# A cross-attention kernel: the order of small steps in its first and last batch

## The chip, the cores and the metric

The kernel runs on one core of a Trainium2 chip. A core has TensorE (PE in the profile; its weight loads are PEld), VectorE (DVE), ScalarE (ACT), GpSimd (POOL) and SyncE (SP); SP only issues DMAs, and ACT and POOL issue some too. All are in-order queues that wait for one another by semaphores. The metric is the device time of one execution in microseconds (us); the median of the runs counts.

## The reference

There are 8 batches; in each, x1 and x2 have 512 channels and 1024 positions, all in float32.

```python
q = jnp.einsum('bcn,dc->bnd', x1, Wq) + bq
k = jnp.einsum('bcn,dc->bdn', x2, Wk) + bk[:, None]
v = jnp.einsum('bcn,dc->bdn', x2, Wv) + bv[:, None]
attn = jax.nn.softmax(jnp.einsum('bnd,bdm->bnm', q, k), axis=2)
attn_out = jnp.einsum('bcm,bnm->bcn', v, attn)
return attn_out + x1
```

Here d is 64. The shapes of Wq and Wk are 64 x 512, that of Wv is 512 x 512.

## The kernel before, in words

**The algebra.** The kernel does not form v. It computes y = x2 times the transposed exponentials of the scores, divides each column by its sum of exponentials, and multiplies by Wv; bv and x1 are added at the end. Both large products are done by seven half-size products instead of eight (the scheme of Strassen and Winograd). The left factor x2 is cut into blocks A11, A12, A21, A22, which are loaded transposed (`load_a`), and four sums S1 to S4 are formed from them (`sum_a`, `left_sums`, `L110`); S3 overwrites A21 and reads A11. The right factor, the exponentials, is cut into blocks "11", "12", "21", "22" with the sums T1 to T4 (`sum_e`, `L262`); T3 overwrites block "12". The products are numbered 1 to 7 (`MULT`). In most batches some of the products 2, 3, 4 and 7 are themselves done by seven smaller products (`inner_left`, `inner_right`, `inner_product`); their sums are at `L355` and `L367`. For product 4 the right inner sums (tile `eI4eT`) are formed from T4. The results of the first stage are y blocks 11, 12, 21, 22 (`evict_y`, `multiply_3` for block 12); the second stage multiplies them with Wv (`second(i)`), and `evict_o` adds bias and x1 and stores.

**The softmax.** Scores lie with keys on the 128 partitions and queries along the row. Half h of the queries has four pairs of score tiles (`scores(s, h, i)`, a pair covering both halves of the keys). Score tiles go from PSUM to SBUF by ScalarE (`L198`, `L200`); the maximum over keys is folded on VectorE (`fold`, `L211`; the two halves at `L215`) and then taken over the partitions by GpSimd (`highest`, `L221`). The subtraction of the maximum is VectorE's (`L243` in the first half of the first batch, `L249` elsewhere), the exponential is ScalarE's (`L244`, `L253`). The sums over keys are folded in the same way (`sums`, or by accumulating DMAs in later batches, `L555`), and reduced over partitions by GpSimd in `total` (`L226`); the reduced row is then brought by a small DMA to a tile `few`, `shares` takes its reciprocal (`L234`), writes it to DRAM (`L236`) and reads it back to all partitions (`L238`) as `rden`.

**The order.** The order of instructions on each engine is written out by hand: `head(s)` prepares the first batch, `head_second` its second half of queries, and `period(s, n, nn, nnn)` does one batch `s` while it prepares the batches `n`, `nn`, `nnn` behind it. In the first batch `s.b == 0`; in the last one `n` is None. Buffers are few: `x` is a single buffer that x1 and x2 of the coming batches take in turn, so a load waits until the queries or keys made from the one before are done. PSUM has two tiles "sc" for scores and inner products and the banks a0, a1, c0, c1 for the large products. Each queue is in order: for example SP issues x2 of batch 1 (`load_x`, `L126`) and then A11 of batch 1 (`load_a`, `L133`).

**T4.** In batches 0 and 1, T4 is formed on VectorE. In the others ScalarE copies block "21" (`L278`) and two DMAs from GpSimd's queue add T2 to the copy (`L280`).

**The last batch.** Near its end stand product 7, product 3 with the eviction of block 12 (`evict_3`: `L452`, then `L483`, which frees the banks a0, a1), and product 4, whose right inner sums (`inner_right(s, 4, ...)`, `L367`) are formed on VectorE after `evict_3`. In `multiply_onto` the first step of product 4 takes T4 itself, the second (number 7) takes the third of these sums.

Of the kernel before, what the change touches and what calls it, by code (L numbers as in the profile page):

```python
# [11 lines left out]
ALU = mybir.AluOpType  # L12
# [3 lines left out]
def kernel(  # L16
# [53 lines left out]
    MH = N // P // 2  # L70
# [64 lines left out]
    def sum_a(s, *ks):  # L135
        for k in ks:
            if k != "S3":
                s.a[k] = sb.tile([P, MH, C // 2], F32, tag=f"a{k}", name=f"a{k}_{s.b}")
        left_sums(s.a, *ks)
# [35 lines left out]
    def scores(s, h, i, bank=None):  # L175


        if i == 0:
            s.e[h] = sb.tile([P, 2, MH, H], F32, tag=f"e{h}", name=f"e_{s.b}_{h}")
        e = s.e[h]  # L180
        if bank:
            whole = None
            ps = [
                ps_a.tile([P, H], F32, tag=f"{bank}{g}", name=f"ps_s{bank}{g}_{s.b}_{h}_{i}")
                for g in range(2)
            ]
        else:
            whole = ps_s.tile([P, 2, H], F32, tag="sc", name=f"ps_s_{s.b}_{h}_{i}")
            ps = [whole[:, g, :] for g in range(2)]
        for g, r in ((0, lo), (1, hi)):  # L190
            nc.tensor.matmul(  # L191
                ps[g], s.k[r, ts(i, P)], s.q[r, ts(h, H)], start=True, stop=True
            )

        def copy():
            if bank:
                for g in range(2):
                    nc.scalar.copy(e[:, g, i, :], ps[g])  # L198
            else:
                nc.scalar.copy(e[:, :, i, :], whole)  # L200

        copy.ps = ps
        return copy

    def fold(s, h, i, kind, op):

        e = s.e[h]
        if i == 1:
            s.mx[h] = sb.tile([P, 2, H], F32, tag="fold", name=f"{kind}_{s.b}_{h}", bufs=2)
        f = s.mx[h]  # L210
        nc.vector.tensor_tensor(f, e[:, :, 0, :] if i == 1 else f, e[:, :, i, :], op)  # L211
# [59 lines left out]
    def sum_t4(s):  # L271

        s.t["T4"] = t4 = sb.tile([P, MH, H], F32, tag="eT4", name=f"eT4_{s.b}")
        if s.b < 2:
            sum_e(s, "T4")
            return
        for i in (0, 2):
            nc.scalar.copy(t4[:, i : i + 2, :], s.t["21"][:, i : i + 2, :])  # L278
        for i in (0, 2):
            nc.gpsimd.dma_start(t4[:, i : i + 2, :], s.t["T2"][:, i : i + 2, :], accum_op=ALU.add)  # L280
# [328 lines left out]
    def head(s):  # L609

        s.q = sb.tile([P, N], F32, tag="q", name=f"q_{s.b}", bufs=2)
        s.k = sb.tile([P, H], F32, tag="k", name=f"k_{s.b}", bufs=2)
        x1_sb = sb.tile([P, CT, N], F32, tag="x", name="x1_head")
        x2_sb = sb.tile([P, 2, MH, H], F32, tag="e1", name="x2_head")
        s.x = x2_sb.rearrange("p a (b t) n -> p (a b) (t n)", t=2)  # L620

        def load_x1(c, h):
            nc.sync.dma_start(
                x1_sb[:, c : c + 2, ts(h, H)],
                x1[s.b, c * P : (c + 2) * P, ts(h, H)].rearrange("(t p) n -> p t n", p=P),
            )

        nc.gpsimd.dma_start(bqk_sb, bqk)
        nc.gpsimd.dma_start(bv_sb, bv)
        nc.scalar.dma_start(wqk_sb, wqk)  # L630
        warm = const.tile([P, P], F32, name="warm")
        nc.vector.memset(warm, 0.0)
        ps = ps_a.tile([P, H], F32, tag="a0", name="ps_warm")
        for _ in range(WARM):
            nc.tensor.matmul(ps[:, 0:P], warm, warm, start=True, stop=True)
        load_x1(0, 0)
        load_x1(2, 0)
        for n in HALVES:
            for c in range(CT):
                to, of = (  # L640
                    x.rearrange("p (h n) -> p h n", h=2)[:, :, n]
                    for x in (s.x[:, c, :], x2[s.b, ts(c, P), :])
                )
                nc.sync.dma_start(to, of)
        nc.scalar.activation(warm[:, 0:1], warm[:, 0:1], AF.Exp)
        load_x1(0, 1)
        load_x1(2, 1)
        load_a(s, "21", "22", "11", "12")
        load_values()
        tiles = range(CT)  # L650
        head_queries(s, x1_sb, 0, "c1")(*tiles)
        head_keys(s, left, "c0")(*tiles)
        more_keys = head_keys(s, right, "a0")
        more_keys(0)
        s.mx[0] = f = sb.tile([P, 2, H], F32, tag="fold", name=f"max_{s.b}_0", bufs=2)
        copies = [scores(s, 0, i) for i in range(2)]
        for g in range(2):
            nc.scalar.copy(s.e[0][:, g, 0, :], copies[0].ps[g])
            nc.vector.tensor_tensor(f[:, g, :], s.e[0][:, g, 0, :], copies[1].ps[g], ALU.max)
        fold_halves(s, 0, ALU.max)  # L660
        more_keys(*tiles[1:])
        copies[1]()
        more_queries = head_queries(s, x1_sb, 1)
        more_queries(0)
        for i, bank in ((2, "a"), (3, "c")):
            copy = scores(s, 0, i, bank)
            for g in range(2):
                nc.vector.tensor_tensor(f[:, 0, :], f[:, 0, :], copy.ps[g], ALU.max)
            copy()
        highest(s, 0, halves=False)  # L670
        sum_a(s, "S1", "S2")
        more_queries(*tiles[1:])
        load_x(states[1], x1)
        copies = [scores(s, 1, 0), scores(s, 1, 1), scores(s, 1, 2, "c")]
        for g in range(2):
            for i in range(MH):
                first_exponentials(s, g, i)
        for copy in copies:
            copy()
        fold(s, 0, 1, "sum", ALU.add)  # L680
        fold(s, 0, 2, "sum", ALU.add)
        fold(s, 1, 1, "max", ALU.max)
        fold(s, 0, 3, "sum", ALU.add)

    def head_second(s, n):


        scores(s, 1, 3)()
        for i in range(2, MH):
            fold(s, 1, i, "max", ALU.max)  # L690
        queries(n)
        load_x(n, x2)
        highest(s, 1)
        sum_a(s, "S3", "S4")
        for i in range(MH):
            exponentials(s, 1, i)

# [10 lines left out]
    def period(s, n, nn, nnn):  # L708
# [15 lines left out]
        if s.b == 0:  # L724
            head_second(s, n)
        sum_e(s, "T1", "T2")
        if s.b < 2:
            total(s, 0)
        else:
            shares(s, 0)  # L730
        if n:
            load_a(n, "11")
        if s.b == 0:
            first(2)
            evict_y(s, "11", (1,))
            keys(n)
            load_x(nn, x1)
            sum_t4(s)
            sums(s, 1)
            shares(s, 0)  # L740
        else:
            evict = multiply_2(s)
            sums(s, 1)
            evict()
            if s.b == 1:
                shares(s, 0)
            sum_t4(s)
            sum_a(s, "S4")
# [37 lines left out]
        if seven:  # L786
            hooks = [{}, {}]
            if n:
                for i in range(MH):
                    lower(n, 0, i)  # L790
                hooks = [
                    {
                        1: lambda: copy_first(n, 0),
                        6: lambda: add_exponential(1),
                        5: lambda: add_exponential(2),
                    },
                    {6: lambda: add_exponential(3)},
                ]
            first(5, (lambda: exponential(n, 0, 0)) if n else None)
            inner_right(s, 3, s.t["22"], "eT1")  # L800
            inner_left(s, 4, s.a["22"], "a12")
            add_7 = multiply_7(s, hooks[0])
            add_7()
            evict_3 = multiply_3(s, hooks[1])
            evict_y(s, "22", (1,))
            evict_3()
            inner_right(s, 4, s.t["T4"], "eT2")
        else:
            first(5)
            if s.b == 0:  # L810
                inner_right(s, 3, s.t["22"], "eT1")
                for i in range(MH):
                    lower(n, 0, i)
            else:
                for i in range(MH):
                    exponentials(n, 0, i)
                start_sum(n, 0)
                inner_right(s, 3, s.t["22"], "eT1")
            first(7)
            if s.b > 1:  # L820
                inner_right(s, 4, s.t["T4"], "eT2")
            evict_3 = multiply_3(s, {})
            if s.b:
                evict_y(s, "22", (1,))
                evict_3()
            else:
                evict_3()
                evict_y(s, "22", (1,))
# [105 lines left out]
```

## Time and profile before

| what | us |
|---|---|
| median of 3 runs | 693.46 (693.18 to 695.86) |
| the profiled execution | 693.62 |
| its span, first to last instruction | 691.8 |
| busy: TensorE / VectorE / ScalarE / GpSimd | 682.8 / 628.9 / 276.1 / 193.5 |
| TensorE's wait for product 4's sums, last batch | 2.3 |
| reductions over partitions: maximum (`L221`, 16 of them) | 1.74 to 2.69, median 2.15 |
| reductions over partitions: sum (`L226`, 16 of them) | 3.18 to 7.54, median 3.98 |

Times in the profile are microseconds from the start of the span. A row of a timeline gives start, duration, engine, line, operation, the tile that is written and those that are read, and, in brackets, how long the engine was idle before it and who ended that. "Landing" is the time from the issue of a DMA until its data are there. The granted clock of TensorE was 1.00 throughout.

### The profile page before, as it was taken

Reading aid. Unit: us, or ns where it says so; the run is one execution under the profiler, and the core shown is the slowest. Engines: PE = TensorE matmul, PEld = TensorE weight load, DVE = VectorE, ACT = ScalarE, POOL = GpSimd, SP = SyncE. Lnnn points to the kernel's source line nnn. Section 1 sums busy time; section 2 is a strip of 40 time slices with the busy share of each in tenths; the row PEclk is TensorE's granted clock in tenths of the full one; section 3 lists DMA queues with packets and bytes.
Section 4 is the critical chain, followed back from the end, with each engine's and each line's share of the span. In section 5 each row is a group of like instructions: output and inputs, shape, how many; then the busy total and the mean of one; then the engine's idle time right before and its main releaser. Section 6 shows DMA issues by size and latency. Waiting matters only on the chain.

```text
span 691.8 us, 6647 instructions
## 1 busy us (share of the span) xinstructions
PE 682.8 (99%) x2248; PEld 364.2 (53%) x2248; DVE 628.9 (91%) x809; ACT 276.1 (40%) x439; POOL 193.5 (28%) x147
## 2 busy tenths in 40 slices
PE   9999999999999999999999999999999999999997
PEld 5333554535545565455644566454754545545753
DVE  1999999988999889998999989999799988999785
ACT  2733353146233552345432454424544245243220
POOL 0123113522423223242142321623223232323000
PEclk9999999999999999999999999999999999999999
DMA  9676256954569754786628867198642864268303
GB/s 304 258 214 238 65 182 130 255 161 79 183 114 235 199 106 153 150 231 181 135 111 180 230 181 187 42 198 215 167 92 38 207 166 76 62 148 223 87 0 122
DMA packets 44723, 109.05 MB, mean 158 GB/s; under 512 B 4880, under 2 KB 7184, under 8 KB 44688
## 3 DMA queue, kind: packets, MB, share of 16 engines
q1 hardware_dynamic: 25856, 70.13, 30.1%
q0 software_dynamic: 17424, 36.25, 29.7%
q10 hardware_dynamic: 1408, 2.23, 1.0%
q8 instruction: 18, 0.29, 0.2%
q14 instruction: 17, 0.14, 0.1%
HBM read 72.62 MB, written 16.81 MB: 129 GB/s over the span
## 4 chain that ended last, share of the span: by engine, by line
PE 93%; DMA 3%; DVE 1%; SPq 1%; ACT 1%; issue 0%; DVEq 0%
PE ps_ya L321 24%; PE ps_i L374 17%; PE ps_oa L321 16%; PE ps_oc L321 12%; PE ps_s L191 6%; PE ps_yc L374 5%; PE ps_q L149 4%; PE ps_k L149 3%; PE ps_yc L321 3%; PE ps_ya L374 3%; DMA a<-in_x2T_dram 1%; DMA x_in_x_dram<-in_x_dram 1%; DMA x_head<-in_x_dram 1%; PE ps_sc L191 1%; PE ps_sa L191 1%; DVE aS L110 0%
## 5 line engine op out<-in xcount | busy, mean ns | idle before, releaser
L321 PE MATMUL ps_ya<-eT,aS 128*128 128x512 f32 x256 | 113.1, 595 | 0.0
L332 ACT COPY uy<-ps_ya 128x512 f32<-128x512 f32 x48 | 28.1, 588 | 139.6 <-PE ps_ya L321 126.7
L249 DVE TENSOR_TENSOR e<-e,top 128x1024 f32<-128x1024 f32 x60 | 70.5, 1228 | 11.0 <-POOL top L221 11.0
L321 PEld LDWEIGHTS ps_ya<-eT,aS 128*128 128x128 f32 x256 | 48.0, 190 | 60.9 <-issue 58.5
L253 ACT ACTIVATE e<-e 128x1024 f32<-128x1024 f32 x60 | 62.9, 1059 | 38.6 <-DVE e L249 37.1
L221 POOL PARTITION_ALL_REDUCE top<-max x16 | 32.8, 2052 | 150.8 <-DVE max L215 78.9
L226 POOL PARTITION_ALL_REDUCE den<-sum x16 | 63.4, 3961 | 40.8 <-DVE sum L215 35.8
L321 PE MATMUL ps_oa<-yT,w_S 128*128 128x512 f32 x128 | 57.6, 593 | 0.0
L321 PE MATMUL ps_oc<-y,w 128*128 128x512 f32 x128 | 57.6, 593 | 0.0
L321 PE MATMUL ps_ya<-e,a 128*128 128x512 f32 x128 | 56.3, 593 | 0.3 <-ACT e L244 0.3
L200 ACT COPY e<-ps_s 128x1024 f32<-128x1024 f32 x46 | 45.7, 1027 | 19.3 <-PE ps_s L191 17.5
L332 ACT COPY uo<-ps_oa 128x512 f32<-128x512 f32 x48 | 27.6, 584 | 54.2 <-PE ps_oa L321 44.9
L383 ACT COPY d<-ps_i 128x256 f32<-128x256 f32 x84 | 29.3, 374 | 47.7 <-PE ps_i L374 47.2
L191 PE MATMUL ps_s<-q,k 64*128 64x512 f32 x188 | 47.3, 608 | 0.8 <-ACT q L590 0.8
L551 POOL DMA_DIRECT2D uo<-in_x_dram x21 | 24.9, 1186 | 79.2 <-DVE uo L548 79.2
L555 POOL DMA_DIRECT2D sum<-e x21 | 25.7, 1222 | 66.5 <-DMA sum<-e 37.0
L321 PEld LDWEIGHTS ps_ya<-e,a 128*128 128x128 f32 x128 | 24.2, 190 | 31.3 <-issue 29.6
L321 PEld LDWEIGHTS ps_oa<-yT,w_S 128*128 128x128 f32 x128 | 24.2, 190 | 30.8 <-issue 29.9
L321 PEld LDWEIGHTS ps_oc<-y,w 128*128 128x128 f32 x128 | 24.1, 190 | 31.0 <-issue 28.9
L211 DVE TENSOR_TENSOR max<-max,e 128x1024 f32<-128x1024 f32 x30 | 36.8, 1225 | 3.0
L507 DVE TENSOR_TENSOR y<-y,den 128x512 f32<-128x512 f32 x54 | 33.8, 683 | 0.0
L238 POOL DMA_DIRECT2D den<-row x16 | 8.9, 557 | 79.0 <-DMA row<-few 73.2
(142 smaller groups left out, 1291.4 us busy)
## 6 DMA issues: line engine op xcount, KB each, us to landing
x_in_x_dram<-in_x_dram SPq DMA_DIRECT2D x60, 512.0 KB, 5.9
a<-in_x2T_dram SPq DMA_DIRECT2D x32, 512.0 KB, 7.1
sum<-e POOLq DMA_DIRECT2D x21, 512.0 KB, 5.2
uo<-in_x_dram POOLq DMA_DIRECT2D x21, 512.0 KB, 6.5
out_dram<-uo SPq DMA_DIRECT2D x21, 512.0 KB, 5.1
eT<-eT POOLq DMA_DIRECT2D x12, 512.0 KB, 6.5
den<-row POOLq DMA_DIRECT2D x16, 256.0 KB, 3.6
r<-in_x_dram POOLq DMA_DIRECT2D x7, 512.0 KB, 8.6
```

The lines of the kernel that those rows point to most:

```text
L149: nc.tensor.matmul(ps[r, :], w_sb[:, c, :], s.x[:, c, ts(h, H)], start=(c == 0), stop=(c == CT - 1),)
L191: nc.tensor.matmul(ps[g], s.k[r, ts(i, P)], s.q[r, ts(h, H)], start=True, stop=True)
L200: nc.scalar.copy(e[:, :, i, :], whole)
L211: nc.vector.tensor_tensor(f, e[:, :, 0, :] if i == 1 else f, e[:, :, i, :], op)
L221: nc.gpsimd.partition_all_reduce(s.top[h], s.mx[h][:, 0, :], P, ReduceOp.max)
L226: nc.gpsimd.partition_all_reduce(s.den[h], s.mx[h][:, 0, :], P, ReduceOp.add)
L249: nc.vector.tensor_tensor(e, e, top, ALU.subtract)
L253: nc.scalar.activation(e, e, AF.Exp)
L321: nc.tensor.matmul(ps[:, n], left[ka][:, k, ts(j, P)], right[kb][:, k, n], start=opens and k == 0, stop=i in (2, 3, 4) and k == n_k - 1, s ...
L332: nc.scalar.copy(s.tmp[i][:, j, :], ps)
L374: nc.tensor.matmul(ps, s.inner[i][ka][:, k, :], s.inner[i, "t"][kb][:, k, :], start=opens and k == 0, stop=z in (2, 3, 4) and k == MH // 2 ...
L507: nc.vector.tensor_tensor(y[:, j, :], y[:, j, :], rden, ALU.mult)
```

## The change

In the first batch: S1 and S2 are formed after the exponentials of the first half of the queries instead of before them; the score pairs 2 and 3 of the second half are computed after product 1 (pair 2 stood before it); the fold of the second maximum stands before the first fold of half 0's sum, and its other two folds of that sum come after T1 and T2; S3 and S4 come after the sums and reciprocal of the halves instead of before the second half's exponentials; A11 of batch 1 is loaded after x1 of batch 2 instead of ahead of product 2; and T4 is formed by the copy and DMAs that the later batches use. In the last batch the right inner sums of product 4 come before the eviction of block 12 (`evict_3`).

```diff
     def sum_t4(s):
...
-        if s.b < 2:
+        if s.b == 1:
             sum_e(s, "T4")
             return
         for i in (0, 2):
             nc.scalar.copy(t4[:, i : i + 2, :], s.t["21"][:, i : i + 2, :])
         for i in (0, 2):
             nc.gpsimd.dma_start(t4[:, i : i + 2, :], s.t["T2"][:, i : i + 2, :], accum_op=ALU.add)
...
         highest(s, 0, halves=False)
-        sum_a(s, "S1", "S2")
         more_queries(*tiles[1:])
         load_x(states[1], x1)
-        copies = [scores(s, 1, 0), scores(s, 1, 1), scores(s, 1, 2, "c")]
+        copies = [scores(s, 1, i) for i in range(2)]
         for g in range(2):
             for i in range(MH):
                 first_exponentials(s, g, i)
         for copy in copies:
             copy()
+        sum_a(s, "S1", "S2")
+        fold(s, 1, 1, "max", ALU.max)
         fold(s, 0, 1, "sum", ALU.add)
-        fold(s, 0, 2, "sum", ALU.add)
-        fold(s, 1, 1, "max", ALU.max)
-        fold(s, 0, 3, "sum", ALU.add)
 
     def head_second(s, n):
...
-        scores(s, 1, 3)()
+        copies = [scores(s, 1, 2, "c"), scores(s, 1, 3)]
+        for copy in copies:
+            copy()
         for i in range(2, MH):
             fold(s, 1, i, "max", ALU.max)
         queries(n)
         load_x(n, x2)
         highest(s, 1)
-        sum_a(s, "S3", "S4")
         for i in range(MH):
             exponentials(s, 1, i)
...
         sum_e(s, "T1", "T2")
+        if s.b == 0:
+            for i in range(2, MH):
+                fold(s, 0, i, "sum", ALU.add)
         if s.b < 2:
             total(s, 0)
         else:
             shares(s, 0)
-        if n:
-            load_a(n, "11")
-        if s.b == 0:
+        if s.b:
+            if n:
+                load_a(n, "11")
+        else:
             first(2)
             evict_y(s, "11", (1,))
             keys(n)
             load_x(nn, x1)
+            load_a(n, "11")
             sum_t4(s)
             sums(s, 1)
             shares(s, 0)
-        else:
+            sum_a(s, "S3", "S4")
+        if s.b:
             evict = multiply_2(s)
...
             evict_y(s, "22", (1,))
-            evict_3()
+            if n:
+                evict_3()
             inner_right(s, 4, s.t["T4"], "eT2")
+            if not n:
+                evict_3()
```

## The prediction

> **What bounds the kernel now.** I read the shares of busy time, then TensorE's own waits, then the chain of waits over the first batch, then the timelines of the two places that the change touches.
>
> ```profile
> span 691.8 us, 6647 instructions
> ...
> PE 682.8 (99%) x2248; PEld 364.2 (53%) x2248; DVE 628.9 (91%) x809; ACT 276.1 (40%) x439; POOL 193.5 (28%) x147
> ```
>
> TensorE sets the time. What an edit can win is the time in which TensorE waits, and the list of its waits is short (us in total, times, longest):
>
> ```profile
> PE ps_i L374 <- DVE eI4eT L367: 2.3, 1, 2.3
> ...
> PE ps_s L191 <- ACT q L590: 0.8, 1, 0.8
> PE ps_ya L321 <- ACT e L244: 0.3, 1, 0.3
> PE ps_i L374 <- ACT e L200: 0.3, 1, 0.3
> ...
> PE ps_k L149 <- DMA x_in_x_dram<-in_x_dram: 0.2, 1, 0.2
> ```
>
> Some 5 us in all. The largest is the last batch's product 4 waiting for its sums (eI4eT). The `L244` and `L149` rows lie in the first batch, whose chain, in order of time, is:
>
> ```profile
> 20.45 1.23 DVE aS L110
> ...
> 21.70 1.95 DVE aS L110
> 23.64 0.61 DVE e L243
> ...
> 24.28 0.64 ACT e L244
> ...
> 24.96 7.13 PE ps_ya L321 x16
> 32.09 1.06 PE ps_s L191 x4
> 33.15 3.61 PE ps_q L149 x16
> ...
> 38.10 8.73 DMA x_in_x_dram<-in_x_dram
> ...
> 46.88 1.08 PE ps_k L149 x4
> 47.95 7.06 PE ps_ya L321 x16
> ```
>
> To be seen: S1, S2 (`L110`) stand before the first exponentials; then TensorE runs through to the queries, whose end frees `x`; the load of x2 for batch 1 is issued then, and its landing holds the keys. After 47.95 TensorE waits for nothing in this batch.
>
> **The last batch.** VectorE does the eviction of block 12 (`L452`, two `L483`) before the four sums `L367`:
>
> ```profile
> 654.49 0.69 DVE L452 TENSOR_TENSOR d<-d,v 128x512 f32<-128x512 f32 x1 [1.16 <-ACT d L383]
> 655.29 1.29 DVE L483 TENSOR_TENSOR y<-ps_ya,d 128x512 f32<-128x512 f32 x2
> 656.49 0.68 DVE L367 TENSOR_TENSOR eI4eT<-eT 128x512 f32<-128x512 f32 x1
> ```
>
> The sums go ahead, into the 1.16 us in which VectorE waited: they start when `evict_y` "22" ends, 653.3. Their input T4 came by DMA issued at 635.25, and the longest landing of `L280` is 10.6, so it is there by 646. Product 4's second step takes the third sum, ready 2.01 after the first one's start (656.49 to 658.50): 655.3. TensorE began product 4 at 655.34 and a step of four takes 0.86, so it wants that sum at 656.20; it got it at 658.65. Won: **2.45**, all of the wait.
>
> What is late next: the eviction of 12 moves behind the sums, to 655.8-657.8. It frees the `a` banks, wanted by `second(1)` at 663.90 - 2.45 = 661.45, and tile `r`, in which ScalarE puts product 4's v at about 657.2 while `L452` has read it by 656.5. From the multiplications by `rden` on VectorE is 1.3 earlier than before (657.7 for 659.02) and TensorE 2.45. The tightest consumer is `second(2)`: y21 was ready at 669.19, now 667.9; TensorE wanted it at 670.77, now 668.32. 0.4 is left. Nothing is given back.
>
> **The head.** S1, S2 leave VectorE while GpSimd takes the maximum over partitions. That reduction took 2.68 from 20.63, and 2.69 from 36.62 in the same company of S3, S4. In batch 2:
>
> ```profile
> 233.25 1.78 POOL L221 PARTITION_ALL_REDUCE top<-max  x1 [6.39 <-DVE few L234]
> 235.07 1.23 DVE L249 TENSOR_TENSOR e<-e,top 128x1024 f32<-128x1024 f32 x1 [1.83 <-POOL top L221]
> ```
>
> These rows of GpSimd's and VectorE's timelines are the case with VectorE idle: 1.78, and VectorE starts 0.04 later. So the first subtraction starts at 20.63 + 1.82 = 22.45 instead of 23.57, product 1 at 23.84 instead of 24.96: 1.12 won. TensorE's two pairs of scores before it end at 23.6. But pair 2 now stands behind product 1: 0.86 (four pairs at 54.95-58.58 are 0.86 to 0.95 each). The queries end 1.12 - 0.86 = **0.26** earlier, and with them the x2 load, its landing (46.6) and product 6 (47.6).
>
> The later A11 load is worth nothing. It is queued behind x2 (issue 38.82, landing 9.3 later, after x2). The x2 load of the next batch, at 62.28 with no A11 behind it, has the same longest landing of 8.7 from its issue. TensorE alone would end the keys at 43.5 + 3.6 = 47.1, so x2 still sets it. In the new place A11 waits for S3 (58.3) and holds A21, A22 in SP's queue; none is used before 113, and x2 of batch 2, queued behind them, is used at 85.8.
>
> **VectorE in batch 0.** S1 and S2 now run at 27.3-29.7, while VectorE would wait for ScalarE's copy of pair 1 (29.8); product 6 needs them at 47.6: no cost. The second maximum: pairs 2 and 3 reach ScalarE by 32.95 (33.20 before), the last fold and halves end at 36.0, and the reduction beside an idle VectorE ends at 37.9. The exponentials of half 1 start at 37.9 instead of 39.56: 1.66 earlier. From there, start to start: four `L249` and the T1, T2 sums 9.33, to 47.2; two folds of half 0's sum, moved here, 2.5; halves 0.7, and GpSimd's den reduction starts at 50.5; two `L502`, to 51.5; three folds of half 1. The first meets the reduction: before, T4's first op met it and ended 3.32 after its start (52.99 - 49.67), so 53.8, then 2.5 and halves 0.7: 57.1. There stand the reciprocal, S3, S4 and T3:
>
> ```profile
> 58.51 4.38 DVE L262 TENSOR_TENSOR e<-e 128x1024 f32<-128x1024 f32 x2
> ```
>
> This row is T3 before: two operations of 1.2 took 4.38, as the second den reduction falls on them. Now S3 and S4 meet it: 4.3 from start to start, then T3 2.3: 63.7, where before it was 62.81. VectorE is **0.85 late**. T4's two operations (3.44 with their stall) are gone, but four others have been put in this stretch. All that follows is as before, up to product 3's inner sums. The third of them (`L367`, 75.26) ended at 75.94, TensorE took it at 76.87. Now 76.8 against 76.61: a wait of 0.3. Then `L483`, which frees `a` for the next scores, ends at 84.1 (83.29), and TensorE wants the bank at 84.0: 0.2. So TensorE goes from 0.26 ahead to **0.25 behind**. Later VectorE waits for TensorE (0.6 and 1.0 before the `L548` at 111.34 and 113.06), and the lateness ends there.
>
> T4 by DMA: two ScalarE copies of 1.04 at about 48.5, where ScalarE idles 2.9; two issues of 1.8 on GpSimd behind few, 54.6-56.4, before the next reduction at 57.1; landing 4.6 to 10.6 later, 67 at worst, used at 69.6. If this cover went, VectorE would wait the difference. Two ends are open for the reciprocal ahead of S3: it waits for few of half 0, issued at 54.0; `L228` lands in 1.8 to 5.9, median 2.3, so 55.8 to 59.9. Up to 59.2 a wait costs nothing, as the reduction would hold S3 as long. I take 57, and keep 0.7 for the range.
>
> **A rule against it.** The trace has VectorE's stalled op waiting 2.1 of the 3.2 of a den reduction (T4's first op, 50.69-52.99, beside 49.67-52.90). The Trainium skill, page "SBUF — State Buffer", section "Who interferes with whom", says that a VectorE instruction with two SBUF inputs and a GpSimd instruction that reads SBUF block each other, the second one for the whole of the first. By it T4's op would have ended at 54.1. Both stalls in the new order would be some 1.2 longer, VectorE 3.3 late, TensorE 2.7 behind, and the sum +0.25: no change. I take the trace.
>
> **Sum.** -2.45 + 0.25 = -2.2. The profiled execution took 693.62 (span 691.8), 0.16 over the median of 693.46: 691.4 for it, **691.3** for the median.
>
> **Rivals.** (a) VectorE is not late at the product 3 sums, as the stalls fall less badly: both gains hold, -2.7, 690.7. For it: 0.85 is the rest of many terms. (b) It is 1 to 2.5 later than I sum (few late, T4's DMA late): TensorE loses the same, 692.3 to 693.8. (c) Slower: the reciprocal. S3, S4, T3 and all of VectorE's queue stand behind it, and T4's 1 MB is put on the same GpSimd queue just behind few. It decides from a landing at 61.4 on (59.2, and the 2.2 of the sum), 7.3 after issue. The other small DMA, `L236`, took up to 8.3: 62.3, 694.4; at `L280`'s longest, 10.6, it is 696.7. Against it: in batches 2 to 7 few also goes out just ahead of `L280` and never took over 5.9. (d) The sums ahead of block 12 do not help, because product 4 meets another wait at once (v's tile, y21): 693.7. Against it: each was looked up above, with 0.4 or more left.
>
> **Numbers.** Forecast 0.65, (a) 0.12, (b) 0.12, (c) 0.07, (d) 0.04. The range goes from 690.0 (a, with the x2 landing a little earlier) to 694.0 (all of b and d), which leaves out c. 0.5% is 3.5 us, about what a measurement of this kernel can tell from no change; my forecast lies inside. Faster needs 689.99: 2.45 and 0.26 and another 0.8, more than the first batch's waits hold: 0.06. Slower needs 696.9, that is (c) at its far end: 0.06.
>
> **What would show it.** The row `L374 <- DVE eI4eT` gone from TensorE's waits; `L221` at 20.6 taking 1.8; product 1 at 23.8; keys still ended by x2, landing at 46.6; T3 of batch 0 ending near 63.7; a wait of some tenths at product 3's first inner sum. I am wrong if VectorE shows a wait at `L234` past 59, or TensorE one over 0.5 between 60 and 100, or one at `second(2)` of the last batch.

## The result, and the profile after

| | before | after | predicted |
|---|---|---|---|
| median of ten runs each, us | 694.24 (693.04 to 697.45) | 692.07 (691.81 to 692.26) | 691.3 from 693.46 |
| profiled execution, us | 693.62 | 692.17 | 691.4 |
| its span, us | 691.8 | 690.4 | |

The ratio is 0.9962, with a 95% interval of 0.9948 to 0.9976: less than the 0.5% that counts as a change, and inside the predicted range. One caution for every median of the kernel before: its executions come at two levels some 2 us apart (693.0 to 694.0, and 694.8 and more), so medians are read here beside the profiled executions, which give -1.45.

The shares of busy time:

```profile
span 690.4 us, 6654 instructions
...
PE 683.3 (99%) x2248; PEld 364.2 (53%) x2248; DVE 626.9 (91%) x807; ACT 277.7 (40%) x441; POOL 190.3 (28%) x149
```

TensorE still sets the time. The list of its waits (us in total, times, longest):

```profile
PE ps_warm L635 <- DVE warm L632: 1.0, 1, 1.0
PE ps_i L374 <- DVE eI3eT L367: 0.8, 1, 0.8
PE ps_s L191 <- ACT q L590: 0.8, 1, 0.8
PE ps_i L374 <- ACT e L200: 0.3, 1, 0.3
PE ps_q L586 <- DMA x_head<-in_x_dram: 0.2, 1, 0.2
```

To be seen: the wait of 2.3 for eI4eT is gone, and so is that of product 1 for `L244`. A new one is there: product 3 of batch 0 waits 0.8 for eI3eT.

**The last batch** did what was forecast. VectorE's timeline:

```profile
654.32 0.68 DVE L367 TENSOR_TENSOR eI4eT<-eT 128x512 f32<-128x512 f32 x1
...
655.65 0.69 DVE L367 TENSOR_TENSOR eI4eT<-eT 128x512 f32<-128x512 f32 x1
...
657.64 1.29 DVE L483 TENSOR_TENSOR y<-ps_ya,d 128x512 f32<-128x512 f32 x2
```

and TensorE's:

```profile
657.27 1.89 PE L374 MATMUL ps_i<-eI4eT,aI 128*128 128x256 f32 x8
...
662.46 3.60 PE L321 MATMUL ps_oa<-y,w 128*128 128x512 f32 x8
```

The sums start as soon as `evict_y` "22" is through, ahead of the `L483` of block 12. The third sum (655.65) is ready at 656.34. Product 4, begun at 656.41, goes on to the step that takes it at 657.27 without a gap, and `second(1)` begins 6.05 after product 4 where before it took 8.56.

**The first batch.** Its chain of waits, from the first reduction on:

```profile
20.98 1.79 POOL top L221
...
24.20 7.13 PE ps_ya L321 x16
31.33 1.06 PE ps_sc L191 x4
...
59.03 3.26 DVE aS L110
62.29 2.27 DVE e L262 x2
...
76.29 1.30 DVE eI3eT L367 x2
77.73 1.97 PE ps_i L374 x8
```

To be seen: the reduction is short (1.79), pair 2 (`ps_sc`) stands before the queries, and the chain then leaves TensorE for VectorE: S4, T3 and everything up to the sums of product 3 (77.73, where before TensorE took that step at 76.87 without waiting).

**Where the time went**, for all kernels run. The same events mark each profiled execution; times in us:

| kernel | first reduction starts | `second(1)` of batch 0 starts | from there to product 4 of the last batch | product 4 to `second(1)` | median, us | ratio (95%) |
|---|---|---|---|---|---|---|
| before | 20.63 | 95.51 | 559.83 | 8.56 | 694.24 | 1 |
| changed | 20.98 | 96.44 | 559.97 | 6.05 | 692.07 | 0.9962 (0.9948, 0.9976) |
| r_changed (the same again) | 20.83 | 96.51 | 559.97 | 6.05 | 692.00 | 0.9960 (0.9948, 0.9972) |
| e1_tail_only | 20.92 | 95.54 | 559.81 | 6.04 | 691.09 | 0.9955 (0.9940, 0.9969) |
| e2_head_only | 20.77 | 96.34 | 559.92 | 8.56 | 694.70 | 1.0007 (0.9996, 1.0017) |
| e3_t4_vector | 20.49 | 99.66 | 559.79 | 6.04 | 697.09 | 1.0034 (1.0020, 1.0048) |
| e4_s34_early | 20.89 | 95.78 | 559.82 | 6.04 | 691.28 | 0.9957 (0.9942, 0.9972) |
| e5_s12_early | 20.84 | 97.60 | 559.91 | 6.05 | 693.28 | 0.9986 (0.9973, 0.9999) |
| e6_a11_early | 20.81 | 95.80 | 559.83 | 6.05 | 691.22 | 0.9949 (0.9937, 0.9961) |
| e7_fold_in_gap | 21.05 | 96.09 | 559.79 | 6.04 | 691.08 | 0.9954 (0.9940, 0.9968) |
| e8_s3_behind_pad | 20.49 | 96.67 | 560.06 | 6.04 | 692.49 | 0.9971 (0.9959, 0.9984) |
| e10_pair2_early | 20.84 | 95.90 | 560.16 | 6.04 | 691.62 | 0.9952 (0.9939, 0.9965) |
| e11_s34_a11_early_gap | 20.48 | 94.92 | 559.84 | 6.05 | 691.05 | 0.9949 (0.9936, 0.9962) |
| e12_long_pad | 21.04 | 96.15 | 559.81 | 6.05 | 691.61 | 0.9957 (0.9944, 0.9970) |

What follows the last column of stretches, to the end of the span, is 27.88 to 27.98 in all of them, and the 560 us in the middle agree within 0.4. So every difference lies in two places: the tail, 2.5 won, and the first 95 us, where the changed kernel gives back 0.9 of it. -2.51 + 0.93 + 0.14 (middle) + 0.04 (end) = -1.40, against spans of 690.4 and 691.8.

### The profile page after: what moved, and what is told of

The parts are those of the page before. It is cut to its first block, busy times and chain, and to the rows that moved or that the text cites. A ratio compares the mean times of both kernels' runs of the same rounds, so it can differ in the third digit from the quotient of the medians.

```text
span 690.4 us, 6654 instructions
## 1 busy us (share of the span) xinstructions
PE 683.3 (99%) x2248; PEld 364.2 (53%) x2248; DVE 626.9 (91%) x807; ACT 277.7 (40%) x441; POOL 190.3 (28%) x149
## 4 chain that ended last, share of the span: by engine, by line
PE 94%; DVE 4%; ACT 1%; DMA 1%; issue 0%; POOL 0%; DVEq 0%; ACTq 0%
PE ps_ya L321 23%; PE ps_i L374 17%; PE ps_oa L321 16%; PE ps_oc L321 12%; PE ps_s L191 5%; PE ps_yc L374 5%; PE ps_k L149 4%; PE ps_q L149 3%; PE ps_yc L321 3%; PE ps_ya L374 3%; PE ps_sa L191 1%; PE ps_sc L191 1%; PE ps_q L586 1%; DMA x_head<-in_x_dram 1%; DVE aI L355 1%; DVE max L211 1%
## 5 line engine op out<-in xcount | busy, mean ns | idle before, releaser
L249 DVE TENSOR_TENSOR e<-e,top 128x1024 f32<-128x1024 f32 x60 | 69.8, 1215 | 12.9 <-POOL top L221 12.9
L221 POOL PARTITION_ALL_REDUCE top<-max x16 | 31.0, 1939 | 149.7 <-DVE max L215 78.8
L226 POOL PARTITION_ALL_REDUCE den<-sum x16 | 60.1, 3756 | 39.0 <-DVE sum L215 38.1
L555 POOL DMA_DIRECT2D sum<-e x21 | 25.8, 1227 | 66.9 <-DMA sum<-e 40.3
L238 POOL DMA_DIRECT2D den<-row x16 | 8.9, 558 | 79.9 <-DMA row<-few 60.4
```

The costliest lines, as they stand in the source:

```text
L221: nc.gpsimd.partition_all_reduce(s.top[h], s.mx[h][:, 0, :], P, ReduceOp.max)
L226: nc.gpsimd.partition_all_reduce(s.den[h], s.mx[h][:, 0, :], P, ReduceOp.add)
L249: nc.vector.tensor_tensor(e, e, top, ALU.subtract)
```

## The experiments

The prediction's own account is called Theory A: the tail wins its whole wait, and the head gives a part back because VectorE comes late to product 3. The rivals put the give-back on few behind T4's DMA (C) or on the A11 load or the x2 load (D), or take it for a difference between executions (B). Each ratio is against the kernel before on the same chip. The pieces of the head were put back one or two at a time; the place of the second maximum's first fold and that of the last fold of half 0's sum were not tried alone.

**1. Tail alone, head alone.** e1 is the kernel before with this edit; e2 is the changed kernel without it:

```diff
-            evict_3()
+            if n:
+                evict_3()
             inner_right(s, 4, s.t["T4"], "eT2")
+            if not n:
+                evict_3()
```

> The kernel before with one edit: in the last batch the sums of product 4 ahead of the eviction of block 12. Theory A (the last batch wins its whole wait, and the first batch's reordering gives 1.0 of it back): TensorE's wait for eI4eT is gone, the span is 2.45 to 2.5 shorter than that of before, about 689.3, so this kernel is faster than the changed one by about 1.0. Rival B (the first batch's edits cost nothing; the 1.07 by which TensorE was late at product 4 in the changed kernel's profile is a difference between executions, since its first matmuls were slow): the same time as the changed kernel within 0.3. On the spread of the runs of before (693.0 to 697.5 where the changed kernel has 691.8 to 692.3): if it comes from the first batch, it stays here; if from the wait in the last batch, it goes.

> The changed kernel with the last batch as before, so only the first batch's edits are in. Theory A: slower than before by about 1.0 (span 692.8 to 692.9), with T3 of batch 0 ending near 64.5, product 3's inner sum near 77.6 and a wait of TensorE of 0.8 there. Rival B: same as before within 0.3. On the spread: if the first batch's edits remove it, the runs lie within 0.5 of each other.

Measured: e1 691.09, e2 694.70. With the tail alone `second(1)` of batch 0 stays at 95.54 and the tail takes 6.04; with the head alone it moves to 96.34 and the tail stays at 8.56. The two parts add up, and the head is a loss of 0.8 to 1.0 (95.51 before; 96.34 in e2, 96.44 and 96.51 in the two profiles of the changed kernel), so B falls. TensorE's waits in e2 have both rows, 2.3 for eI4eT and 0.8 for eI3eT. The ratio of e2, 1.0007, does not show the loss, because the kernel before had more executions with a lowered clock (see 3): with a mean granted clock of 0.999 or more, e2 took 694.0 to 695.0 and the kernel before beside it 693.4 to 693.7.

One part of the expectation was a miss: e2's runs did not draw closer together (694.0 to 696.89). e1's did, but for one (690.81 to 691.48, and 693.13), so the spread belongs in the main to the wait in the last batch.

**2. S3, S4 back beside the second maximum; A11 back as well (e6).**

```diff
         highest(s, 1)
+        sum_a(s, "S3", "S4")
         for i in range(MH):
             exponentials(s, 1, i)
...
             shares(s, 0)
-            sum_a(s, "S3", "S4")
```

In e6, moreover, `load_a(n, "11")` stands where the kernel before has it.

> The changed kernel with S3 and S4 back ahead of the exponentials of half 1, beside the second maximum's reduction. Theory A (VectorE's order in batch 0 sets the loss: S3, S4 cost 2.3 more where they were put, and 1.1 where they were): reduction 2.7 and S4 2.0 again, exponentials of half 1 at 39.8, but T3 ends near 63.4 instead of 64.5, TensorE's wait at product 3 is 0 to 0.1, span 0.8 to 1.0 shorter than the changed kernel, about 689.5. Rival B (VectorE's order there does not matter to TensorE): same as the changed kernel within 0.3.

> As the kernel with S3 and S4 back, and A11 of batch 1 loaded at its old place too, behind x2 in SP's queue. Theory A (transfers of one queue land in order, so A11 behind x2 takes nothing from it): keys end within 0.1 of the kernel with S3 and S4 back alone, same time within 0.3. Rival D (A11 shares the bandwidth with x2): x2's last landing 0.6 to 1.3 later and the time with it.

Measured: 691.28 and 691.22; `second(1)` at 95.78 and 95.80. VectorE's timeline in e4:

```profile
39.75 4.62 DVE L249 TENSOR_TENSOR e<-e,top 128x1024 f32<-128x1024 f32 x4
...
59.44 4.04 DVE L262 TENSOR_TENSOR e<-e 128x1024 f32<-128x1024 f32 x2
```

Here the two sums put the exponentials (`L249`) at 39.75, 1.03 later than in the changed kernel (38.72). At their late place they cost more: T3 ends at 63.41 in e4 and at 64.49 in the changed kernel. So 2.1 is paid late for 1.03 saved early, even though the den reduction's stall falls on S4 there and on T3 (4.04) here. That is the give-back: 0.7 of it disappears with this move. Not all of it: TensorE still waits 0.43 at product 3, where 0 to 0.1 was expected. The profile names a copy of ScalarE for this wait, but the third sum ends at 76.91, 0.15 before the step starts, as in the changed kernel (77.58 and 77.73). The A11 load's place is worth nothing (95.78 and 95.80), so D falls as far as A11 goes.

**3. T4 of batch 0 on VectorE again.**

```diff
-        if s.b == 1:
+        if s.b < 2:
             sum_e(s, "T4")
```

> The changed kernel with T4 of batch 0 on VectorE again (two operations of 1.2). Theory A (VectorE's lateness in batch 0 passes to TensorE at product 3, microsecond for microsecond, once the slack of 0.9 there is used up): VectorE 2.4 later, TensorE's wait at product 3's inner sum 0.8 + 2.4 = 3.2, time 2.4 longer than the changed kernel. Rival C (the DMAs of T4 on GpSimd's queue cost as much as they save, since they delay few, the den reduction or the row): the same time within 0.5, with the reciprocal or the reduction earlier by 1 or more.

Measured: `second(1)` at 99.66, 3.2 later than in the changed kernel, and the profiled execution took 695.19. TensorE waits 3.0 for eI3eT, expected 3.2. The DMA for T4 pays, since VectorE is the engine that is late. few landed 1.9 after its issue without T4 in the queue and 2.0 with it, so C falls.

Only half of the 3.2 is VectorE's lateness. The first row is from TensorE's timeline in e3; the second is the stretch from 79.58 to 83.00, with its length, TensorE's busy time and matmuls, the granted clock, the DMA engines' share and GB/s:

```profile
79.26 3.44 PE L374 MATMUL ps_i<-eI3eT,aI 128*128 128x256 f32 x8 [2.99 <-DVE eI3eT L367]
```

```profile
79.58:83.00 3.42, 3.42 (x10) 0.50 0.39 77
```

The step starts 1.53 later than in the changed kernel (77.73). Then its eight matmuls take 3.44 instead of 1.97, as the granted clock is 0.50 for 3.4 after the wait, and from this step to `second(1)` it is 20.40 instead of 18.71: 1.69 more.

The mean granted clock is on record for each execution, and it explains most of the two levels of the kernel before. Of its 52 executions beside the experiments, 27 have 0.997 or 0.998; their median is 695.17. The other 25 have 0.999 or 1.000; their median is 693.46, which is 1.71 less, and half the clock for 3.4 costs 1.7. Apart from the kernel before only e2 (4 of 12) and e3 (all 8) have executions below 0.999. These are the three kernels in which TensorE waits 2.3 or 3.0 in one piece; the 78 executions of all the others have none. So the two moved lines of the tail seem to win twice, the wait itself and a lowered clock that followed it in half of the executions. The clocks of e1 (none lowered of 6) and e2 tie the second part to the tail's edit; that the wait lowers the clock there is inferred, as e3 alone has a trace with the lowered clock. The ratios contain it, as 12 of 17, 9 of 24 and 6 of 11 executions of the kernel before had it on the three chips.

**4. S1, S2 back beside the first maximum.**

```diff
         highest(s, 0, halves=False)
+        sum_a(s, "S1", "S2")
...
             copy()
-        sum_a(s, "S1", "S2")
```

> The changed kernel with S1 and S2 back ahead of the exponentials, beside the first maximum's reduction. Theory A: the reduction takes 2.7 instead of 1.8, the first subtraction comes 1.1 later, everything behind it in batch 0 too (S1 and S2 had been in idle time), TensorE's wait at product 3 stays near 0.8 as TensorE and VectorE are late alike, time 1.1 longer than the changed kernel. Rival D (x2's load, issued when the queries end, sets TensorE, and the queries end 0.9 later): 0.9 longer. If moving S1 and S2 does nothing: same time.

Measured: 693.28, 1.2 more than the changed kernel. GpSimd's timeline:

```profile
20.84 2.68 POOL L221 PARTITION_ALL_REDUCE top<-max  x1 [18.35 <-DVE max L668]
```

The reduction takes 0.90 longer, the first subtraction starts at 23.78 and product 1 at 25.17. Counted from the reduction's start, product 1 is 1.11 later than in the changed kernel, where 1.12 was forecast: this part of the head is a gain. TensorE's wait at product 3 is 1.2 (near 0.8 was expected), so VectorE sets that point here too, and not x2's load.

**5. The late copies of pair 2.** In the changed kernel VectorE is idle for 0.97 at 32.5, the maximum fold of pair 2 waiting for ScalarE's copies. e7 moves a fold of the sum from behind T1 and T2 into that gap; e10 starts pair 2's scores ahead of product 1 again:

```diff
         fold(s, 0, 1, "sum", ALU.add)
+        fold(s, 0, 2, "sum", ALU.add)
...
-            for i in range(2, MH):
-                fold(s, 0, i, "sum", ALU.add)
+            fold(s, 0, 3, "sum", ALU.add)
```

```diff
-        copies = [scores(s, 1, i) for i in range(2)]
+        copies = [scores(s, 1, 0), scores(s, 1, 1), scores(s, 1, 2, "c")]
...
-        copies = [scores(s, 1, 2, "c"), scores(s, 1, 3)]
-        for copy in copies:
-            copy()
+        scores(s, 1, 3)()
```

> The changed kernel with one of the two folds of half 0's sum put back ahead of the second maximum's last folds, where VectorE stood idle 0.97 for ScalarE's copies. Theory A: exponentials of half 1 some 0.3 later, the stretch behind them 1.25 shorter, product 3's inner sum near 76.6, TensorE's wait there 0 to 0.1, time 0.7 to 1.0 shorter than the changed kernel (about 691.2). Rival B (VectorE's order in batch 0 does not set TensorE): same within 0.3.

> The changed kernel with score pair 2 of half 1 computed before product 1 again (its copies by ScalarE then follow the exponentials at once, as before). Theory A: product 1 starts 0.6 to 0.7 later, as TensorE's third pair ends only at 24.5, but only one pair stands behind it, so the queries and x2's landing move by -0.2 at most; pair 2's copies are there by 31.9 instead of 33.5, VectorE's gap of 0.97 goes, and the exponentials of half 1 start only 0.1 to 0.3 earlier, since pair 3's copy then sets them. TensorE's wait at product 3 stays within 0.3 of the changed kernel, the time within 0.4. If the late pair 2 is what made VectorE late, the time is 0.8 shorter.

VectorE's timeline in the changed kernel:

```profile
33.53 2.55 DVE L211 TENSOR_TENSOR max<-max,e 128x1024 f32<-128x1024 f32 x2 [0.97 <-ACT e L198]
```

and in e10:

```profile
37.94 4.63 DVE L249 TENSOR_TENSOR e<-e,top 128x1024 f32<-128x1024 f32 x4 [1.91 <-POOL top L221]
```

e10 took 691.62 against 692.00 of the changed kernel beside it: -0.4. Its fold waits 0.52 instead of 0.97, and one copy earlier; its exponentials start at 37.94, which is what the prediction had written (37.9) for a pair 2 behind product 1. The reduction starts at the same time in the two (20.84 and 20.83), so the 0.63 between 37.94 and 38.57 is pair 2's copy. The expectation of 0.1 to 0.3 was too low.

e7 took 691.08, 0.9 less than the changed kernel as expected, but not in the expected way: TensorE still waits 0.7 for eI3eT where 0 to 0.1 was expected. The reason is in VectorE's timeline, a new wait of 0.50 at batch 1's third maximum fold:

```profile
66.55 1.22 DVE L211 TENSOR_TENSOR max<-max,e 128x1024 f32<-128x1024 f32 x1 [0.50 <-ACT uy L332]
```

VectorE, 1.0 earlier at T3's end (0.8 against r_changed), came ahead of ScalarE's copy and lost half of it. `second(1)` is 0.4 earlier than in r_changed; the rest of the 0.9 between the medians is not located by this one profile, which is of a run at the high end of e7's (691.62).

**6. What in the reduction collides with VectorE.** A VectorE operation that has begun before a maximum reduction stretches it from 1.78 to 2.68. Could S3 begin a little after it and be free? e8 puts one small memset between, e12 three:

```diff
+    pad = const.tile([P, 384], F32, name="pad")
...
         highest(s, 1)
+        nc.vector.memset(pad, 0.0)
+        sum_a(s, "S3")
...
-            sum_a(s, "S3", "S4")
+            sum_a(s, "S4")
```

> The changed kernel with S3 put beside the second maximum's reduction, but behind a memset of a spare tile (0.4 us, no input), so that GpSimd's reduction starts before S3 does; S4 stays late. Theory L (whoever starts first holds the other, and the reduction holds VectorE only for its first 0.85): the reduction stays at 1.8, S3 takes 2.0 to 2.1, exponentials of half 1 at 39.1 instead of 38.7, the later stretch 1.2 shorter, TensorE's wait at product 3 near 0, time 0.7 shorter than the changed kernel. Rival S (the second one is blocked for the whole of the first): S3 takes 2.7, exponentials at 39.9, time 0 to 0.2 shorter. Rival T (the two share, whatever the order): reduction 2.2 or more.

> The changed kernel with S3 beside the second maximum's reduction, behind three memsets instead of one, so that S3 would start about 1.0 after the reduction. With one memset S3 started 0.24 after the reduction and the reduction took 3.0. Theory P (the reduction reads SBUF only in a part of its run that begins later than 0.24 after its start; outside of it the two don't meet): reduction 1.8, S3 starts up to 1.0 behind it and takes 1.2 to 1.6, exponentials of half 1 0.1 to 0.6 later than in the changed kernel, T3 of batch 0 0.6 to 1.1 earlier, time 0.5 to 0.9 shorter. Rival S (the second to start is held for the whole of the first): S3 ends 1.2 after the reduction, exponentials 1.2 later, no gain.

GpSimd, then VectorE, in e8 (line numbers are 2 higher):

```profile
36.41 3.03 POOL L223 PARTITION_ALL_REDUCE top<-max  x1 [14.14 <-DVE max L217]
```

```profile
36.65 1.16 DVE L112 TENSOR_TENSOR a<-a,a 128x1024 f32<-128x1024 f32 x1
```

and in e12:

```profile
36.96 1.78 POOL L223 PARTITION_ALL_REDUCE top<-max  x1 [14.14 <-DVE max L217]
```

```profile
38.24 1.16 DVE L112 TENSOR_TENSOR a<-a,a 128x1024 f32<-128x1024 f32 x1
```

In e8 S3 starts 0.24 after the reduction, runs its full 1.16 undisturbed, and the reduction takes 3.03, the longest maximum reduction seen here: starting later did not put VectorE behind. T's "2.2 or more" came, but not by sharing, since S3 was not slowed. e8's exponentials start at 39.48, and its `second(1)` at 96.67 is later than the changed kernel's although its first reduction began 0.49 earlier. In e12 S3 starts 1.28 after the reduction's start, 0.5 before its end, and neither is disturbed; the exponentials follow at 39.32. This fits a reduction of which only a part collides with VectorE's sums, a part that begins later than 0.24 and is over by 1.28 after its start; it is inferred from these cases, not seen. e12 is 0.4 faster than r_changed, less than was expected (0.5 to 0.9), and T3 ends 0.2 earlier instead of 0.6 to 1.1: with fewer operations ahead of it, VectorE's reciprocal now waits 1.86 for few, 4.9 after its issue at 55.48:

```profile
60.37 0.18 DVE L236 RECIPROCAL few<-few 128x4 f32<-128x4 f32 x1 [1.86 <-DMA few<-den]
```

**7. The changed kernel again, and the pieces that paid, together.** e11 is e6 with e7's edit.

> The changed kernel once more, beside the three others of this call, so that they are compared on one chip: 690.1 to 690.5 in span, TensorE's wait at product 3's inner sum 0.6 to 0.9.

> The changed kernel with S3, S4 and A11's load back at their old places and one fold of half 0's sum back in VectorE's gap. Theory A: VectorE reaches product 3's inner sums 1.3 or more earlier than in the changed kernel, TensorE waits for nothing there, span 689.0 to 689.5, time 0.9 to 1.4 shorter than the changed kernel. Rival: the gain of the two edits is not additive and the kernel stays at 689.6, because TensorE is then held by x2's landing alone.

r_changed: 692.00, its wait for eI3eT 1.1 (expected 0.6 to 0.9), `second(1)` at 96.51. e11: 691.05, TensorE with no wait at product 3 at all and `second(1)` at 94.92, the earliest of all fourteen. VectorE's third sum of product 3 starts at 74.24 there and TensorE takes it at 76.28. The span of 688.7 was a little below the 689.0 to 689.5 expected; its first reduction also started 0.35 earlier than r_changed's. It beats the kernel before by 0.51% (ratio 0.9949, 0.9936 to 0.9962; 0.35% against that kernel's median with the clock not lowered) and, in the same comparison, has a median 0.95 below the changed kernel's; the intervals of the two ratios overlap. Nor do the medians tell it from the tail edit alone (691.05 and 691.09): almost all that was found in this change is its two moved lines at the end. e10's edit was not put together with these.

## Why the prediction was right, and which term was off

The time came out 0.8 above the predicted median, well in the range, and it is no change beyond 0.5%, to which the prediction gave 0.88 (all but the 0.06 and 0.06). The medians of the result differ by 2.17, and -2.2 was forecast; that agreement is luck. With the clock lowered in neither kernel the change is -1.4 (692.07 against 693.46), and the forecast knew nothing of the lowered clock.

**The tail, -2.45: right.** Product 4 to `second(1)` went from 8.56 to 6.05, and e1 shows it alone. Nothing was late next: the `L505` that ends y21's multiplications is through at 669.0, TensorE goes on at 669.32 without a wait. The spare was 0.3 where 0.4 was written. Rival (d) is out.

**S1, S2 moved, reduction 1.78: right.** It took 1.78, and its start to product 1 took 3.22, forecast 3.21. Product 1 itself began at 24.20 and not at 23.84, because the first reduction began 0.35 later in this execution, in code that is the same in both kernels (see the last point below).

**Queries and x2: right, and worth little.** The x2 load's first issue came at 36.88, 0.25 earlier than before once the 0.35 is taken off; it landed at 46.74 and product 6 began at 47.79, 0.1 earlier. A later start was absorbed there in e1 too: with its reduction 0.29 later than before's, x2 landed at 46.86 against 46.83. So the start of an execution does not simply add to its end.

**A11: nothing, right** (e6 against e4). **T4 by DMA hidden: right**: issued at 55.44 and 56.00, landed by 64.29, used at 71.5; without it product 3's step is 1.5 later and `second(1)` 3.2, with the lowered clock (e3). **few ahead of the reciprocal, rival (c): did not come.** It was issued at 54.88 and landed at 56.92, in 2.0; the worst of the experiments, 60.4 in e12, still is short of the 61.4 from which it decides.

**The stalls beside the den reductions: the trace's size, not the rule's.** In the changed kernel, GpSimd:

```profile
51.35 3.24 POOL L226 PARTITION_ALL_REDUCE den<-sum  x1 [12.66 <-DVE sum L215]
...
58.02 4.20 POOL L226 PARTITION_ALL_REDUCE den<-sum  x1 [0.75 <-DVE few L234]
```

and VectorE:

```profile
52.37 2.30 DVE L211 TENSOR_TENSOR sum<-e 128x1024 f32<-128x1024 f32 x1
...
59.03 3.26 DVE L110 TENSOR_TENSOR aS<-a,aS 128x1024 f32<-128x1024 f32 x1
```

The fold ended at 54.67, 0.1 after the first reduction, and S4 at 62.29, 0.1 after the second. Had each been held for the whole of the reduction, as the rule of the Trainium skill ("SBUF — State Buffer", "Who interferes with whom") was read in the prediction, both would have ended 1.1 later, at 55.8 and 63.4. That reading is a strict one: the section calls the shared port an exclusive lock and says of two SBUF inputs that they contend, and its "for the whole instruction" stands beside VectorE's two-port modes. The prediction's "waiting 2.1 of the 3.2" counts from the reduction's start; T4's operation itself was 1.1 late, like the fold here. From the first `L249` of half 1 to the end of T3 the sum said 25.8; it took 25.77, in both profiles of this kernel.

**The mis-sized term: where that stretch begins.** "The exponentials of half 1 start at 37.9" is the step that failed. They started at 38.72: 0.35 is this execution's start, the other 0.47 the step "the last fold and halves end at 36.0". From the start of the two folds to the end of the halves it is 3.28, so 36.0 has the folds start near 32.7; they started at 33.53, or 33.18 without the 0.35. The prediction took pairs 2 and 3 to reach ScalarE by 32.95 and counted only the order; but pair 2's matmuls end at 32.39, its two copies on ScalarE at 33.50, and VectorE stood idle for 0.97 in front of its fold. e10, with pair 2 ahead, starts the exponentials at 37.94, and r_changed, whose first reduction began 0.20 later than before's, at 38.57. All that follows was shifted by it: T3's end 64.49 for 63.7, third sum of product 3 at 77.58 for 76.8, and TensorE's wait 0.8 (1.1 in r_changed) for 0.3. The wait of 0.2 for the bank that `L483` frees did not come. The give-back "0.25 behind" became 0.93 at `second(1)` and 1.07 at product 4 of the last batch. Rival (b), VectorE "1 to 2.5 later" than summed, was nearer in size (0.8 later, and its 692.3 is 0.2 from the result), but not in its causes: neither few nor T4 was late.

Still open: some executions lie 1.3 us or more above their kernel's median with the clock not lowered (four of the kernel before, two of e5, one each of e1, e4, e11 and e12). No trace of one was kept. Open too is why the clock was lowered in some executions of the kernel before and not in others.

## What to carry to other kernels

Work that stretches a reduction can still be cheap there: S3 and S4 cost 1.03 beside it and 2.1 later, where their engine was already the late one. Sum the whole stretch up to the next point at which the bounding engine waits, and ask for every fold or copy whether its input is there, not only whether its turn has come. When a change has two ends far apart, mark the same three or four events in both traces: it took one table to see that the tail's two lines brought all of the gain and the rest a small loss. Look at the granted clock of each execution, too: a long wait of TensorE can cost more than its length, as in e3.

## What the runs showed of the hardware that was not expected

- A maximum reduction over partitions (128x512 float32) takes 1.78 alone, 2.68 with VectorE in the middle of a sum of two SBUF tiles at its start (the sum behind that one took 1.94 to 2.06 instead of 1.22), 3.03 with one starting 0.24 after it, and 1.78 again with one starting 1.28 after it. VectorE's operation was undisturbed at 1.16 in the last two.
- The VectorE operation that began 1.0 after the start of a den reduction of 3.24, or of 4.20, took 1.1 or 2.1 longer than alone and ended 0.1 after the reduction, and so did one that began 1.9 after the start of a reduction of 3.23 (e12): it took 0.24 longer. The 4.20 has a sum of VectorE under way at its start; without one it is 3.23 (e4, e12).
- After a wait of 2.99 TensorE's granted clock was 0.50 for 3.4 (e3). Executions with a mean clock below 0.999 come only from the three kernels with a wait of 2.3 or 3.0.
- The first reduction started between 20.48 and 21.05 in fourteen executions whose code is the same up to there. In the changed kernel's execution the head's first 16 matmuls took 4.23 from 5.90, before's took 3.65 from the same 5.90. The rows show a clock of 1.00 for both, but the trace's table of the granted clock begins only at 7.12 in the changed kernel and at 5.52 in the kernel before. In six of the fourteen traces it begins 0.2 to 1.2 after these matmuls do, and they take 3.71 to 4.23, longer by about half of that stretch (0.58 for 1.22); in the other eight it begins earlier, and they take 3.65. That fits half the clock until the table begins; the table itself has no value there.
